# A graph kernel's closing part written out operation by operation, with two additions moved to VectorE

## The chip, the cores and the metric

One core of one Trainium2 chip runs the whole kernel in one launch. The metric is the device time of that core in microseconds (us). Three runs of the kernel before gave 239.44, 239.58 and 240.66 us; their median is 239.58 us.

## The reference, cut to what matters

Two layers over a 0/1 adjacency matrix of 4096 x 4096 and features `x` of 4096 x 64. Each ends in a layer normalisation of the residual sum.

```
# layer 0: neighbours weighted by 0.5^(k - pos), pos = running count of neighbours in the row
w   = mask * where(pos > 0, 0.5 ** (k - pos), 0)
x1  = layernorm(x + w @ (x @ W0) + b0)
# layer 1
deg = max(sum(adj, axis=1) + 1, 1)
z   = concat([x1, (adj @ x1 + x1) / deg]) @ W + b
r   = relu(z)
out = layernorm(x1 + r / max(norm(r, axis=1), 1e-12))
```

Layer 1 needs all rows of `x1`, so the last rows of layer 0 and much of layer 1 are left for the end. That end is what is changed here.

## The kernel before

**Tiling.** The 4096 rows are cut into 8 slabs of 512 (index g), each slab's 4096 neighbours into 8 pieces of 512 (index k). A piece of the transposed adjacency is a bf16 tile of 128 x 4 x 512, brought in by a DMA that GpSimd issues. The main loop walks 64 such pieces. For each it counts neighbours, turns counts into weights (ScalarE line 294, VectorE line 295) and sums layer 0 on TensorE (line 305, `gather`). As soon as a slab's `x1` is known, TensorE also takes in layer-1 sums for other slabs (line 314, `second`), which are set aside in `part`.

**The closing part** begins when the loop ends, at about 193 us of the trace. Slab 7's layer 0 is finished first: `first_hT`, `first_pz` (line 414), then on VectorE the sum y, mean and variance (`moments`, lines 387 and 389), the root (`root_a` and `root_b`, lines 358 to 368) and `x1` (line 441), then a high and a low fp16 half of it (lines 446, 450, 453). The low half is needed by every piece with k = 7.

Next TensorE does the pieces of layer 1 that are left. `own(g, k)` adds one piece to slab g's bank: four matmuls of 512 columns. `own_half(h, k)` (line 608) does the same with 256 columns for half h of slab 7. When a slab has its last piece, `last_hT` (line 627, VectorE) or `half_hT` (line 632, ScalarE) empties the bank into `hT`, and `last_pz` (line 659, TensorE, fp32) multiplies `hT` with the weights.

**A unit** is what follows for one slab, two slabs (4 and 5, 0 and 1) or half of slab 7. Its steps, in order:

- `last_z` (line 664, VectorE) adds the own-row term c1 to the product.
- `last_relu` and `last_sq` (668, 673, ScalarE; 675, VectorE for the halves) and `last_ss` (680, 681, VectorE) give the row's sum of squares.
- `last_rn` gives the inverse norm: a power on GpSimd (line 378), for the halves a root on ScalarE and four small VectorE operations.
- `last_y` (698, VectorE), then `last_add` (703), which adds `x1`: on GpSimd for whole slabs, on VectorE for halves.
- `last_mv`: four or eight times `bn_stats` (387) and then as many `bn_aggr` (389).
- `last_r` (376, 378) and `offset` (736, 737) on GpSimd give scale and offset, `last_o` (748, ScalarE) the output block by block, and `store` (757) hands it to the DMA queue of SP.

Slabs 3 and 7 share one last root (`u37`), so that both wait for the last half; their output is split between VectorE (750) and ScalarE (748).

**What sets the order.** The scheduler is told to keep the written order: each engine executes its instructions in the order in which the closing part calls these functions. Only semaphores stand between the engines. Within one function all instructions of it stand together: the eight `bn_stats` of a unit are issued in one row.

**Buffers.** Small results have tiles of their own from a pool with five buffers for each tag. PSUM banks are kept in a list: a bank emptied goes to the end and the next user takes the first. Outputs and intermediate tiles of the units reuse the buffers of adjacency pieces.

Of the kernel before, what the change touches and what calls it, by code (L numbers as in the profile page):

```python
# [23 lines left out]
P = 128  # L24
# [16 lines left out]
def adj_resnorm_kernel(  # L41
# [583 lines left out]
    def last_hT(g):  # L625
        ep["hT", g] = hT_of(g)
        nc.vector.tensor_tensor(ep["hT", g], acc[g], part[g], ALU.add)  # L627
        banks.append(acc[g])
# [7 lines left out]
    def unit(*slabs):  # L636
        name, bs = "_".join(map(str, slabs)), [g * TB + t for g in slabs for t in range(TB)]
        n = len(bs)
        tiles = []
        for i in range(n // TB):  # L640
            tiles.append(a16p.tile([P, 4 * TB // n, n, D], F32, tag="a16", name=f"u_{name}_{i}"))
        four = [t[:, i] for t in tiles for i in range(4 * TB // n)]
        return name, bs, four

    def half_unit(h):
        _, bs, four = u7
        ts_ = slice(2 * h, 2 * h + 2)
        return f"{L}{'ab'[h]}", bs[ts_], [f[:, ts_] for f in four]

    def rows(bs):  # L650
        return slice(bs[0], bs[-1] + 1)

    def last_pz(u):

        name, bs, _ = u
        pz = ep["pz1", name] = psum(len(bs), D, f"pz1_{name}")
        for t, b in enumerate(bs):
            h = ep["hT", b // TB]
            nc.tensor.matmul(pz[:, t, :], lhsT=h[:, ts(b % TB, P)], rhs=wn_sb, start=True, stop=True)  # L659

    def last_z(u):

        name, bs, (z, _, _, _) = u
        nc.vector.tensor_tensor(z, ep["pz1", name], c1[:, rows(bs), :], ALU.add)  # L664
        free(f"pz1_{name}")

    def last_relu(u):
        nc.scalar.activation(u[2][1], u[2][0], AF.Relu)  # L668

    def last_sq(u):  # L670
        name, bs, (z, sq, _, _) = u
        if len(bs) >= TB:
            nc.scalar.activation(sq, sq, AF.Square)
        else:
            nc.vector.scalar_tensor_tensor(sq, z, 0.0, z, ALU.max, ALU.mult)

    def last_ss(u):
        name, bs, (_, sq, _, _) = u
        ss = ep["ss", name] = small.tile([P, len(bs)], F32, tag="ss", name=f"ss_{name}")
        nc.vector.tensor_reduce(ss, sq, AX.X, ALU.add)  # L680
        nc.vector.tensor_tensor(ss, ss, least[:, rows(bs)], ALU.max)  # L681

    def last_sn(u):
        name = u[0]
        ep["sn", name] = root_a(ep["ss", name], zero, f"n_{name}")

    def last_rn(u):
        name = u[0]
        ss = ep["ss", name]
        if ("sn", name) in ep:  # L690
            ep["rn", name] = root_b(ep["sn", name], ss, zero, f"n_{name}")
        else:
            ep["rn", name] = root_p(ss, None, name, "rn")

    def last_y(u):
        name, bs, (z, _, y, _) = u
        rn = ep["rn", name].unsqueeze(2).to_broadcast([P, len(bs), D])
        nc.vector.scalar_tensor_tensor(y, z, 0.0, rn, ALU.max, ALU.mult)

    def last_add(u):  # L700
        name, bs, (_, _, y, _) = u
        engine = nc.gpsimd if len(bs) >= TB else nc.vector
        engine.tensor_tensor(y, y, x1[:, rows(bs), :], ALU.add)

    mv_37 = small.tile([P, 2 * TB, 2], F32, tag="mv_37", name="mv_37")
    slot_of = {3: 0, L: TB}

    def last_mv(u):
        name, bs, (_, _, y, _) = u
        if bs[0] // TB in slot_of:  # L710
            ep["mv1", "37"] = mv_37
            t = slot_of[bs[0] // TB] + bs[0] % TB
            moments(y, f"l1_{name}", mv_37[:, t : t + len(bs), :])
        else:
            ep["mv1", name] = moments(y, f"l1_{name}")

    def last_s(u):
        name = u[0]
        ep["s1", name] = root_a(ep["mv1", name][:, :, 1], eps_ln, f"l1_{name}")

    def last_r(u):
        name = u[0]
        v = ep["mv1", name][:, :, 1]
        if ("s1", name) in ep:
            ep["r1", name] = root_b(ep["s1", name], v, eps_ln, f"l1_{name}")
        else:
            ep["r1", name] = root_p(v, LN_EPS, name, "r1")

    def offset(u):
        name, bs, _ = u  # L730
        mv, r = ep["mv1", name], ep["r1", name]
        off = ep["off", name] = small.tile([P, len(bs)], F32, tag="off", name=f"off_{name}")
        if ("s1", name) in ep:
            nc.vector.scalar_tensor_tensor(off, mv[:, :, 0], -1.0, r, ALU.mult, ALU.mult)
        else:
            nc.gpsimd.tensor_tensor(off, mv[:, :, 0], r, ALU.mult)
            nc.gpsimd.tensor_scalar(off, off, -1.0, None, ALU.mult)

    def last_o(u, t0, t1, engine=nc.scalar):
        name, bs, (_, _, y, o) = u  # L740
        if bs[0] // TB in slot_of:
            n0 = slot_of[bs[0] // TB]
            mv, r, off = [ep[what, "37"][:, n0 : n0 + TB] for what in ("mv1", "r1", "off")]
        else:
            mv, r, off = ep["mv1", name], ep["r1", name], ep["off", name]
        for t in range(t0, t1):
            if engine is nc.scalar:
                engine.activation(o[:, t, :], y[:, t, :], AF.Identity, bias=off[:, t : t + 1], scale=r[:, t : t + 1])
            else:
                engine.tensor_scalar(  # L750
                    o[:, t, :], y[:, t, :], mv[:, t, 0:1], r[:, t : t + 1], ALU.subtract, ALU.mult
                )

    def store(u):
        name, bs, (_, _, _, o) = u
        for i, b in enumerate(range(0, len(bs), TB)):
            nc.sync.dma_start(out=out[bs[b] // TB], in_=o[:, b : b + TB, :])

    run(NS, DVE)
    gather(*held)  # L760
    own(5, 5)
    first_hT(L)
    banks.append(ps_a.tile([P, R], F32, tag="acc0", name="va0"))
    first_pz(L)
    own(5, 6)
    first_y(L)
    first_mv(L)
    own(4, 6)
    free(f"pz0_{L}")
    first_s(L)  # L770
    own(0, 6)
    first_least(L)
    first_r(L)
    own(1, 6)
    first_x1(L)
    own(2, 5)
    first_hi(L)
    own_half(1, 0)
    first_xl(L)
    own(6, 6)  # L780
    first_lo(L)
    own(6, 7)
    own(4, 7)
    last_hT(6)
    u6 = unit(6)
    last_pz(u6)
    last_hT(4)
    own(5, 7)
    last_z(u6)
    last_relu(u6)  # L790
    own(1, 7)
    last_hT(5)
    last_sq(u6)
    last_ss(u6)
    own(0, 7)
    last_hT(1)
    last_rn(u6)
    u45 = unit(4, 5)
    last_pz(u45)
    last_hT(0)  # L800
    last_y(u6)
    last_add(u6)
    u01 = unit(0, 1)
    last_pz(u01)
    last_z(u45)
    last_mv(u6)
    last_relu(u45)
    last_sq(u45)
    last_r(u6)
    own(2, 7)  # L810
    last_z(u01)
    last_ss(u45)
    own(2, 6)
    last_relu(u01)
    offset(u6)
    last_sq(u01)
    first_px(L)
    last_rn(u45)
    own(3, 7)
    last_hT(2)  # L820
    first_x1T(L)
    free(f"px_{L}")
    last_ss(u01)
    u2 = unit(2)
    last_pz(u2)
    last_o(u6, 2, 4)
    last_o(u6, 0, 2)
    last_y(u45)
    last_rn(u01)
    first_pu(L)  # L830
    last_z(u2)
    store(u6)
    own(3, 6)
    last_relu(u2)
    first_c1(L)
    free(f"pu_{L}")
    last_sq(u2)
    last_add(u45)
    own_half(1, 6)
    last_y(u01)  # L840
    own_half(1, 7)
    last_ss(u2)
    own(3, 5)
    last_add(u01)
    last_mv(u45)
    own_half(1, 1)
    own_half(1, 4)
    last_rn(u2)
    own_half(1, 3)
    own_half(1, 2)  # L850
    last_hT(3)
    own_half(1, 5)
    last_r(u45)
    last_y(u2)
    u3 = unit(3)
    last_pz(u3)
    last_mv(u01)
    half_hT(1)
    u7 = unit(L)
    u7b = half_unit(1)  # L860
    last_pz(u7b)
    own_half(0, 1)
    last_add(u2)
    last_z(u3)
    own_half(0, 7)
    last_z(u7b)
    last_relu(u3)
    own_half(0, 6)
    last_sq(u7b)
    offset(u45)  # L870
    last_ss(u7b)
    own_half(0, 2)
    last_sq(u3)
    last_r(u01)
    own_half(0, 0)
    last_o(u45, 4, 6)
    last_ss(u3)
    own_half(0, 3)
    last_mv(u2)
    last_sn(u7b)  # L880
    own_half(0, 5)
    last_o(u45, 6, 8)
    own_half(0, 4)
    last_rn(u7b)
    last_o(u45, 2, 4)
    last_rn(u3)
    last_y(u7b)
    half_hT(0)
    last_add(u7b)
    last_o(u45, 0, 2)  # L890
    u7a = half_unit(0)
    last_pz(u7a)
    last_y(u3)
    offset(u01)
    last_z(u7a)
    last_add(u3)
# [69 lines left out]
```

## Time and profile before

| | value |
|---|---|
| median of 3 runs | 239.58 us |
| the profiled execution's own time | 239.75 us |
| its span in the trace | 238.0 us |
| outside the span | 1.75 us |
| closing part: last `gather` matmul ends, to the end of the span | 193.13 to 238.0 us |
| busy time in the span: PE, DVE, ACT, POOL | 211.8, 180.1, 136.2, 83.3 us |
| from 193.13 to 227.92 us (34.79 us): PE busy | 32.27 us |
| mean granted TensorE clock over the span | 0.971 |

PE is TensorE, PEld its weight loads, DVE is VectorE, ACT is ScalarE, POOL is GpSimd, SP is the engine that issues the stores. A timeline row gives start, length, engine, line, operation, output and inputs, shapes and the count of instructions in it; in brackets stands the idle time in front of it and who ended it. A row with x4 covers four instructions that follow each other, so that its length divided by four is their spacing and not the duration of one. In the chain of waits, a row gives the part of that work that the end of the span hung on. The granted clock is a share of full speed.

### The profile page before, as it was taken

Reading aid. Unit: us, or ns where it says so; the run is one execution under the profiler, and the core shown is the slowest. Engines: PE = TensorE matmul, PEld = TensorE weight load, DVE = VectorE, ACT = ScalarE, POOL = GpSimd, SP = SyncE. Lnnn points to the kernel's source line nnn. Section 1 sums busy time; section 2 is a strip of 40 time slices with the busy share of each in tenths; the row PEclk is TensorE's granted clock in tenths of the full one; section 3 lists DMA queues with packets and bytes.
Section 4 is the critical chain, followed back from the end, with each engine's and each line's share of the span. In section 5 each row is a group of like instructions: output and inputs, shape, how many; then the busy total and the mean of one; then the engine's idle time right before and its main releaser. Section 6 shows DMA issues by size and latency. Waiting matters only on the chain.

```text
span 238.0 us, 7425 instructions
## 1 busy us (share of the span) xinstructions
PE 211.8 (89%) x3128; PEld 98.4 (41%) x3171; DVE 180.1 (76%) x457; ACT 136.2 (57%) x205; POOL 83.3 (35%) x160
## 2 busy tenths in 40 slices
PE   8689979889997999999999999999999999996920
PEld 2223324234433533443345344434453354765810
DVE  5459788987896699778847975686768765789973
ACT  6058876788676756653655456555645521171582
POOL 8344573432432311213221152214610000277940
PEclk9799999999999999999999999999999999999795
DMA  6999999999999999999999999999930000000021
GB/s 200 209 216 220 212 213 212 222 215 213 220 213 215 214 222 213 212 213 218 218 208 186 193 206 185 187 178 183 196 77 3 3 0 0 3 1 23 3 88 66
DMA packets 11985, 37.34 MB, mean 157 GB/s; under 512 B 1328, under 2 KB 3504, under 8 KB 11952
## 3 DMA queue, kind: packets, MB, share of 16 engines
q0 software_dynamic: 9216, 33.56, 72.4%
q1 hardware_dynamic: 2736, 3.31, 4.5%
q8 instruction: 25, 0.41, 0.6%
q14 instruction: 8, 0.07, 0.1%
HBM read 69.37 MB, written 1.05 MB: 296 GB/s over the span
## 4 chain that ended last, share of the span: by engine, by line
PE 47%; DMA 34%; issue 7%; DVE 7%; POOL 2%; ACT 2%; ACTq 0%; POOLq 0%
DMA a<-in_adjT_dram 34%; PE acc L305 11%; PE acc_part L314 10%; PE v L278 5%; PE cnt L248 4%; PE v L287 3%; PE va L659 2%; PE va L314 2%; PE vb L608 2%; PE pi L528 2%; PE rep L266 1%; PE vb L314 1%; PE ma L314 1%; PE pz L414 1%; ACT w L294 1%
## 5 line engine op out<-in xcount | busy, mean ns | idle before, releaser
L294 ACT ACTIVATE w<-v,less 128x1024 int16<-128x1024 f32 x64 | 71.3, 1113 | 50.4 <-PE v L287 38.0
L295 DVE TENSOR_SCALAR w<-v 128x1024 int16<-128x1024 f32 x64 | 78.2, 1222 | 19.1 <-PE v L287 17.7
L105 POOL DMA_DIRECT2D a<-in_adjT_dram x64 | 35.8, 560 | 97.0 <-PE rep L266 34.4
L305 PE MATMUL acc<-w,xhl 128*128 128x512 bf16 x240 | 66.1, 379 | 2.1 <-issue 1.1
L314 PE MATMUL acc_part<-a,x1hl 128*128 128x512 bf16 x132 | 37.3, 381 | 2.1 <-issue 1.4
L305 PEld LDWEIGHTS <-xhl 128*128 128x128 f16 x256 | 23.1, 98 | 32.7 <-issue 9.1
L268 ACT ACTIVATE near<-rep,most 128x512 bf16<-128x512 f32 x39 | 26.6, 682 | 8.2 <-PE rep L266 8.1
L314 PEld LDWEIGHTS <-x1hl 128*128 128x128 f16 x224 | 18.6, 98 | 30.4 <-issue 14.4
L278 PE MATMUL v<-a,tri 32*32 32x512 bf16 x1024 | 28.7, 385 | 0.5 <-ACT w L294 0.5
L287 PE MATMUL v<-near,mine 32*32 32x512 bf16 x1024 | 27.7, 376 | 0.0
L248 PE MATMUL cnt<-a,pick 128*32 128x512 bf16 x256 | 21.2, 386 | 6.5 <-DMA a<-in_adjT_dram 4.9
L258 DVE TENSOR_TENSOR cs<-cnt,cs 128x512 bf16<-128x512 f32 x31 | 21.2, 685 | 6.4 <-PE cnt L248 6.3
L278 PEld LDWEIGHTS <-tri 32*32 32x32 bf16 x1024 | 9.7, 88 | 19.7 <-issue 19.3
L378 POOL TENSOR_TENSOR rn<-ss,power 128x4 f32<-128x4 f32 (+1 forms) x5 | 6.3, 1276 | 29.0 <-DVE ss L681 28.9
L266 PE MATMUL rep<-cs,further 128*128 128x512 bf16 x39 | 15.0, 385 | 1.0 <-DVE cs L258 1.0
L248 PEld LDWEIGHTS <-pick 128*32 128x32 bf16 x256 | 6.0, 94 | 21.5 <-issue 12.6
L233 POOL TENSOR_TENSOR a<-a,ident_b 128x128 bf16<-128x128 bf16 x32 | 12.7, 429 | 0.1
L287 PEld LDWEIGHTS <-mine 32*32 32x32 bf16 x1024 | 10.3, 87 | 2.5 <-issue 2.4
L659 PE MATMUL va<-wts,hT 128*128 128x64 f32 x64 | 8.8, 292 | 2.4 <-DVE hT L627 1.9
L260 DVE CAST cs<-cnt 128x512 bf16<-128x512 f32 x8 | 5.5, 691 | 6.7 <-PE cnt L248 6.7
L659 PEld LDWEIGHTS va<-wts,hT 128*128 128x128 f32 x64 | 8.4, 206 | 3.7 <-DVE hT L627 2.8
L668 ACT ACTIVATE u<-u 128x256 f32<-128x256 f32 (+1 forms) x5 | 2.5, 502 | 12.4 <-DVE u L664 12.4
(136 smaller groups left out, 241.5 us busy)
## 6 DMA issues: line engine op xcount, KB each, us to landing
a<-in_adjT_dram POOLq DMA_DIRECT2D x64, 512.0 KB, 16.5
c<-in_x_quads_dram SPq DMA_DIRECT2D x2, 512.0 KB, 4.5
x<-in_x_dram SPq DMA_DIRECT2D x8, 128.0 KB, 7.3
out_dram<-u SPq DMA_DIRECT2D x8, 128.0 KB, 1.7
wts<-in_weights_dram SPq DMA_DIRECT2D x1, 160.0 KB, 7.2
```

The source lines that it names most:

```text
L105: nc.gpsimd.dma_start(out=a, in_=adjT[g, k])
L248: nc.tensor.matmul(cnt[g][quarters[q], :], lhsT=pick[:, PW - 4 * k : PW - 4 * k + Q], rhs=A[g][k][:, q, :], start=first, stop=last,)
L258: nc.vector.tensor_tensor(new, cnt[g], cs[g], ALU.add)
L266: nc.tensor.matmul(pr, lhsT=further, rhs=cs[g], start=True, stop=True)
L268: nc.scalar.activation(near[g], pr, AF.Relu, bias=most, scale=-1.0)
L278: nc.tensor.matmul(v[e // 2][quarters[q], e % 2, :], lhsT=tri[quarters[e], :], rhs=A[g][k][quarters[e], q, :], start=True, stop=False,)
L287: nc.tensor.matmul(v[e // 2][quarters[q], e % 2, :], lhsT=mine[quarters[e], 4 * k + q, :], rhs=nr[quarters[e], :], start=False, stop=True,)
L294: nc.scalar.activation(w[:, 0:2, :], v[0], AF.Relu, bias=less)
L295: nc.vector.tensor_scalar(w[:, 2:4, :], v[1], -STEP * MAX_NEIGH, 0.0, ALU.add, ALU.max)
L305: nc.tensor.matmul(acc0[g], lhsT=xhl[:, b, :], rhs=w[:, q, :].bitcast(BF16), start=(k, q) == (NK - 1, 0), stop=(k, q) == (0, KB - 1),)
L314: nc.tensor.matmul(acc, lhsT=x1hl[:, b, :], rhs=A[g][b // KB][:, b % KB, :], start=first, stop=last)
L659: nc.tensor.matmul(pz[:, t, :], lhsT=h[:, ts(b % TB, P)], rhs=wn_sb, start=True, stop=True)
```

## The change

The calls of the closing part are replaced by a table `work` of named single operations and a written `order` of names; each name is issued once, in that order. So the instructions of one unit no longer stand together: `bn_stats` and `bn_aggr` of several units are mixed with each other and with additions, and the pieces of TensorE come in another sequence. The arithmetic is the same with three differences: the sum `y + x1` of slabs 2 and 3 goes from GpSimd to VectorE (`DVE_ADDS`); GpSimd takes the sign of the mean as a first step and multiplies by the scale afterwards (before: product, then sign); of slab 7's last four blocks VectorE does three and ScalarE one (before two and two). All small results lie in one tile `scratch`, in columns of their own. The store of slab 3 is issued in front of slab 7's (before: behind it). The main loop is not touched.

```diff
-    def last_add(u):
-        name, bs, (_, _, y, _) = u
-        engine = nc.gpsimd if len(bs) >= TB else nc.vector
-        engine.tensor_tensor(y, y, x1[:, rows(bs), :], ALU.add)
...
-            nc.gpsimd.tensor_tensor(off, mv[:, :, 0], r, ALU.mult)
-            nc.gpsimd.tensor_scalar(off, off, -1.0, None, ALU.mult)
...
+    scratch = a16p.tile([P, KB * R // 2], F32, tag="a16", name="scratch")
+    taken = [0]
+    def little(n, m=None):
+        v = scratch[:, taken[0] : taken[0] + n * (m or 1)]
+        taken[0] += n * (m or 1)
+        return v if m is None else v.rearrange("p (n m) -> p n m", m=m)
...
+    def statistics(name, y, mv):
+        st = little(mv.shape[1], 6)
+        for t in range(mv.shape[1]):
+            work[f"bn_{name}_{t}"] = lambda t=t: nc.vector.bn_stats(st[:, t, :], y[:, t, :])
+            work[f"ag_{name}_{t}"] = lambda t=t: nc.vector.bn_aggr(mv[:, t, :], st[:, t, :])
...
+    UNITS = ['6', '45', '01', '2', '3', '7b', '7a']
+    COPIED = ()
+    DVE_ADDS = ('2', '3', '7b', '7a')
+    SHARED = ('3', '7b', '7a')
...
+        adder = nc.vector if u in DVE_ADDS else nc.gpsimd
+        work["add" + u] = lambda: adder.tensor_tensor(y, y, x1[:, rows, :], ALU.add)
+        statistics(u, y, mv)
...
+                by_dve = tt >= (1 if u in halves else 2)
...
+        work["eps" + u] = lambda: nc.gpsimd.tensor_scalar(r1, mv[:, :, 1], LN_EPS, None, ALU.add)
+        work["pow" + u] = lambda: nc.gpsimd.tensor_tensor(r1, r1, power[:, 0:n], ALU.pow)
+        work["neg" + u] = lambda: nc.gpsimd.tensor_scalar(off, mv[:, :, 0], -1.0, None, ALU.mult)
+        work["of" + u] = lambda: nc.gpsimd.tensor_tensor(off, off, r1, ALU.mult)
...
+    order = """
+        gather own5_6 fhT fpz own0_6 y0 bn_L0_3 bn_L0_0 own1_6 bn_L0_1 bn_L0_2 ag_L0_0 ag_L0_2 ag_L0_3 ag_L0_1
+        deg s0 own2_6 qa_r0 qb_r0 qc_r0 least qd_r0 own5_5 x1_1 x1_2 x1_3 x1_0 own6_6 least2 hi xl own4_6 lo
+        own6_7 own4_7 hT6 own5_7 hT4 pz6 hT5 pz45 z6 relu6 sq6 ss6 own0_7 ssm6 z45 rn6 own1_7 relu45 hT0 y6 sq45
+        px ownha_6 hT1 add6 x1T ownha_0 ss45 pz01 ssm45 bn_6_1 rn45 ag_6_1 bn_6_0 ag_6_0 bn_6_2 ag_6_2 bn_6_3 pu
+        ag_6_3 z01 own2_5 eps6 y45 relu01 pow6 own2_7 t1 sq01 c1 own3_6 add45 ss01 own3_5 hT2 ssm01 bn_45_5 rn01
+        bn_45_6 pz2 bn_45_3 bn_45_4 ag_45_3 bn_45_2 bn_45_1 bn_45_0 own3_7 ag_45_0 ag_45_6 ag_45_4 ag_45_1 z2
+        y01 neg6 ownha_2 relu2 of6 ownhb_5 o6_1 ag_45_5 ag_45_2 add01 bn_45_7 sq2 ownha_4 ag_45_7 hT3 o6_2
+        ownhb_1 o6_0 ss2 pz3 o6_3 eps45 ssm2 bn_01_6 bn_01_0 st6_0 rn2 bn_01_5 bn_01_7 ownha_7 bn_01_2 ag_01_7
+        bn_01_1 ownha_5 ag_01_6 z3 neg45 ownha_1 y2 relu3 pow45 bn_01_4 ownhb_0 bn_01_3 sq3 add2 ownha_3 bn_2_0
+        bn_2_2 ownhb_4 ag_2_0 bn_2_1 hT7a ss3 pz7a of45 ssm3 bn_2_3 o45_1 ag_01_5 rn3 ownhb_3 ag_01_1 ag_01_2
+        ag_01_3 ag_01_0 o45_0 ag_01_4 ag_2_3 ownhb_6 ag_2_1 z7a o45_5 ownhb_7 sq7a o45_2 eps01 y3 ownhb_2 o45_3
+        neg01 ss7a pow01 o45_7 st45_0 ssm7a ag_2_2 add3 hT7b sn7a bn_3_0 pz7b o45_6 bn_3_2 bn_3_1 bn_3_3 o45_4
+        qa_n7a z7b qb_n7a st45_4 of01 sq7b qc_n7a o01_3 neg2 ss7b eps2 ag_3_1 o01_0 ag_3_0 ssm7b ag_3_3 pow2
+        qd_n7a sn7b y7a o01_5 qa_n7b add7a o01_4 qb_n7b bn_7a_0 o01_7 qc_n7b of2 ag_7a_0 bn_7a_1 qd_n7b o2_3 y7b
+        o2_0 ag_7a_1 ag_3_2 add7b o2_2 bn_7b_1 bn_7b_0 o01_6 ag_7b_1 ag_7b_0 sS st01_4 o01_2 qa_S qb_S o2_1 qc_S
+        o01_1 qd_S st2_0 offS o7_3 o3_1 st01_0 o3_3 o3_2 o3_0 o7_1 o7_0 st3 o7_2 st7
+    """
     run(NS, DVE)
...
+    for name in order.split():
+        work.pop(name)()
```

The names: `ownG_K` a piece of slab G, `ownha_K` and `ownhb_K` of slab 7's first and second half, `hTU` the emptying of a bank, `pzU` the fp32 product, then `zU`, `reluU`, `sqU`, `ssU` and `ssmU` (sum of squares and its floor), `rnU` (inverse norm by GpSimd's power) or `snU` and `qa_` to `qd_` (by a root), `yU`, `addU`, `bn_` and `ag_` (statistics), `epsU`, `powU`, `negU`, `ofU` (scale and offset), `oU_T` one output block, `stU` a store. `sS`, `qa_S` to `qd_S` and `offS` are the root and offset shared by slabs 3 and 7.

## The prediction

> **What bounds the kernel now.** I read the share of slices first: the only slices in which TensorE is neither busy nor at full clock lie at the end, so the closing part from 193.13 us was read row by row. TensorE's timeline there has one long hole:
>
> ```profile
> 215.81 2.35 PE L608 MATMUL mb<-a,x1hl 128*128 128x256 bf16 x20
> 220.09 2.32 PE L659 MATMUL va<-wts,hT 128*128 128x64 f32 x12 [1.94 <-DVE hT L627]
> 222.21 4.58 PE L608 MATMUL vb<-a,x1hl 128*128 128x256 bf16 x32
> 227.25 0.66 PE L659 MATMUL va<-wts,hT 128*128 128x64 f32 x4 [0.46 <-ACT hT L632]
> ```
>
> TensorE stood 1.94 us for the emptying of slab 3's bank. Its work behind the hole was also slow: 32 matmuls of 256 columns took 4.38 us in the chain, where the 20 in front took 2.35 us with the pipeline's end (109 ns apart). The windows (PE's busy time, then the granted clock) say why:
>
> ```profile
> 218.50:219.50 1.00, 0.00 (x0) 1.00 0.00 0
> 220.50:221.50 1.00, 1.00 (x8) 0.58 0.00 0
> 221.50:222.50 1.00, 1.00 (x7) 0.50 0.00 0
> 222.50:223.50 1.00, 1.00 (x7) 0.50 0.00 0
> 223.50:224.50 1.00, 1.00 (x8) 0.71 0.00 0
> 224.50:225.50 1.00, 1.00 (x11) 1.00 0.06 16
> ```
>
> Why was the bank emptied late? The chain that ended last runs through VectorE in front of it:
>
> ```profile
> 214.71 1.76 DVE u L698
> 216.47 0.34 DVE ss L680
> 216.81 0.02 issue
> 216.84 1.07 DVE ss L681
> 217.90 1.02 DVE st_l L387 x8
> 218.92 0.54 DVE mv_l L389 x8
> 219.47 0.58 DVE hT L627
> ```
>
> Two rows are too long: line 698 on 128x512 takes 0.69 us elsewhere, line 681 takes 0.16. And 16 statistics stand in front of line 627, though TensorE needs that one. GpSimd's timeline shows what ran beside the two long rows:
>
> ```profile
> 214.51 1.41 POOL L703 TENSOR_TENSOR u<-u,x 128x512 f32<-128x512 f32 x1
> 216.62 1.27 POOL L703 TENSOR_TENSOR u<-u,x 128x512 f32<-128x512 f32 x1 [0.69 <-DVE u L698]
> ```
>
> Line 681 ends with the second addition, line 698 about half a microsecond after the first.
>
> **What the Trainium skill says.** SBUF — State Buffer, section Who interferes with whom: a VectorE instruction with two SBUF inputs and a GpSimd instruction that reads SBUF exclude each other, and the later one waits for all of the earlier; one with a single SBUF input, and a reduction, do not. The two rows above agree, and so does line 627 (one input in PSUM), which took its usual 0.69 us during GpSimd work. GpSimd's powers do not show it: line 681 took 0.17 us at 212.57 inside a power of 1.64 us. TensorE: Matmul & The Clock Gate, section What's actually happening: an idle window of about 3.4 us halves the clock. Here 1.94 us were enough; the low clock lasted about 3.4 us. The same page, Architectural detail, has VectorE and ScalarE as strict queues, which the trace bears out: nothing overtakes. VectorE: DVE Perf Modes, The DRAIN you can't avoid, holds that a wait between two VectorE operations costs nothing extra. This trace differs: independent `bn_stats` follow each other every 128 ns though one lasts 208, while each step of a root starts only 20 to 30 ns after its predecessor's end. So mixing steps of different units saves some 0.1 us a step.
>
> **The change, part by part.** I wrote down the new order for each engine and walked it with the rows of before: an instruction starts when its engine is free and its inputs are there, plus the 0.03 to 0.08 us that the trace shows between engines. Spacings: piece 0.862, half piece 0.436, fp32 product of a slab 0.88 (two blocks alone 0.66), output block on ScalarE 0.345, `bn_aggr` 0.067.
>
> *TensorE, same instructions in another sequence.* The end of the gather stays at 193.13. The first trap is own6_7, which needs the low half of x1: its VectorE and ScalarE steps are unchanged (ready at 200.06), and one piece, the product of 0.99 and six pieces bring TensorE to 200.17, so nothing is lost, with 0.1 us to spare (before: 0.5). Then three pieces and 12 blocks of product (205.5), two pieces, transpose 0.22 and two halves (208.3), product of slabs 0 and 1 (210.1), pu 0.23, four pieces, product of slab 2 (214.65), own3_7 (215.5) and four halves: TensorE comes to pz3 at 217.3. It needs hT3. On VectorE z2 runs 214.9 to 215.3, y01 waits for rn01 (GpSimd, ready 215.36) and ends at 216.1, three small statistics follow, hT3 runs 216.4 to 217.1. So the hole of 1.94 us closes, with 0.15 us to spare, because statistics of units 0 and 1 now stand behind hT3. With the hole goes the low clock: 3.4 us at half clock is 1.7 us of work. Six halves, pz7a (its wait for hT7a hides behind the sixth, ownhb_4) and four halves end at 223.2; hT7b (0.37 on ScalarE, whose six output blocks in front of it are through at 223.2) and 0.66 us of product end at 224.3, before 227.92. Gain up to here: 1.94 + 1.7 = 3.64 us, and the wait of about 0.46 us for the last hT stays.
>
> *The additions.* Adding x1 to slabs 2 and 3 costs VectorE 2 x 0.42 us (the row of c1, same shape and inputs) and frees GpSimd of 2 x 0.73. The two left on GpSimd lie, in the walk, at 212.2 to 213.5 and 216.15 to 217.4. Beside them VectorE has reductions, statistics and bank emptyings; only ssm01 and ssm2 have two SBUF inputs and come right at their end. So about 2.0 us of blocking (1.76 - 0.69 and 1.07 - 0.16) become at most 0.2. That feeds the closing of the hole and is not counted again.
>
> *GpSimd.* Its list of powers and offsets, 19.57 us busy from 205.58 before, loses 1.46 and keeps 18.1; with 0.07 us between instructions and 1 to 1.5 us of waits it ends at 226.6 instead of 229.5. The sign in front of the power costs nothing and gains nothing by itself, since GpSimd does its four steps in a row either way: it moves 0.25 us from behind the power to in front of it. Where the mean waits for nothing, that is a gain of 0.25 us for the first output block; where GpSimd is the late engine, zero. I take zero.
>
> *The tail.* From z7b (224.34): square, sum, floor 225.4; root on ScalarE 225.8; four small operations 226.56; y, add, two `bn_stats`, two `bn_aggr` 227.75. The shared root sS is ready to start at 227.8, but on ScalarE it stands behind seven output blocks (225.75 + 7 x 0.345 = 228.2). Root 0.3, four small operations, offset: 229.6. Then three blocks on ScalarE: 230.75. Before, the same point was 235.05 and the span ended 2.95 us later (store issue 0.33, landing 1.7, end). The other stores are issued earlier than before, and slab 3's just ahead of slab 7's, which finds SP's queue free again 0.33 us later, about when its last block is done. So the span would end at 233.7. Against the 3.64 us above this is 0.66 us more: one ScalarE block fewer at the end (0.34), and slab 3's statistics no longer between floor and root (about 0.4), less the wait of sS.
>
> *Sum.* 238.0 - 3.64 - 0.66 = 233.7. The walk has almost no slack on three engines at once, and none of its small hand-offs was allowed to be late. I add 0.4 us for that: a choice, about a dozen hand-offs at 0.03. Span 234.1, plus 1.75 outside gives 235.85 for an execution like the profiled one, which lay 0.17 above the median: **235.7**.
>
> **The rivals.** *(B) GpSimd becomes the bound.* Offset of slab 2 is ready at 226.6 and ScalarE wants it at 226.8; sS queues behind it. If GpSimd runs 1 to 2 us later than walked, sS and the end move by nearly as much: 236.7 to 238.3, say 237.2. For it: 18 of 20.8 us busy. Against: before, it had 4.4 us of idle in its list, so its rows are true durations. *(C) The hole comes back smaller,* at pz3 or at pz01, where the product needs hT1: an idle time of 1.5 to 2 us with the low clock again leaves only the tail's 0.7 and some of the addition's: 238.4 to 240. *(D) Slower.* hT3 stands behind y01, and y01 behind GpSimd's pow6, add45 and rn01. If these run 2.5 us later than walked, TensorE waits 2.4 us at 217.3, and its remaining 7 us begin with 3.4 us at half clock (1.7); with about 1 us that the late engines add to the tail this comes to 5.1: 240.8. A delay below some 2.4 us doesn't make it slower than before. Against it: GpSimd's two powers in front are 1.05 and 1.64 in five and four rows, with little spread. *(E) One shared tile makes engines wait for each other.* If dependencies were kept for the tile and not for columns, VectorE's statistics would wait for GpSimd's powers. In the built order they wait only for VectorE and for the addition; I leave it within D.
>
> **Chances.** Walk as described 0.68 (own range 234.6 to 236.6), B 0.19, C 0.07, D with E 0.06. The range 234.6 to 237.8 leaves out C, D, the end of B and a little below. Half a per cent, about what a measurement of this kernel can tell, is 1.2 us: faster means under 238.4. Faster 0.87, same 0.07, slower 0.06.
>
> **What would show it.** Right: no idle time of over 0.7 us on PE from 193 to 224 and clock 1.00 there; PE's last product at about 224.3; GpSimd's last row at 226 to 227; sS on ScalarE near 228.2; no VectorE row on line 777 over 0.8 us or on 776 over 0.3. Wrong: a hole in front of a line 757 product with a clock near 0.5 after it, or VectorE idle for GpSimd in front of y.

## The result

The kernel after takes 237.04 us, the median of seven runs (236.68 to 238.51); seven runs of the kernel before on the same chip gave 239.58 (238.34 to 240.66). The ratio is 0.9919, with a 95% interval of 0.9892 to 0.9946: faster, by 2.5 us between the medians or about one per cent. Ratios, intervals and spans here and below are taken from the fast runs of each kernel, so that a ratio is not the quotient of the two medians beside it. In a later series it was 236.93 us against 239.82, a ratio of 0.9869 (0.9834 to 0.9905). The forecast was 235.7, a gain of 3.9 us in a range of 234.6 to 237.8.

The profiled execution took 238.51 us with a span of 235.0; the spans of the others are 234.7 to 235.8, so its closing part is a typical one, and only the time outside the span is long in it. In the kernel after, line 757 is the fp32 product, 710 and 715 empty the banks, 777 is y, 775 and 776 the sum of squares and its floor, 774 the inverse norm's power, 781 the addition, 804 to 807 the steps `eps`, `pow`, `neg` and `of` of GpSimd, 788 the output, 768 a half's root, 827 the shared root, and 649 and 650 `bn_stats` and `bn_aggr`.

The granted clock in the page of the kernel after, in 40 slices:

```profile
PEclk9999999999999999999999999999999999999995
```

TensorE's timeline of the kernel after (start, length, engine, line, operation, tiles and shapes, count; idle time in front):

```profile
217.73 1.10 PE L757 MATMUL vb<-wts,hT 128*128 128x64 f32 x8 [0.24 <-DVE hT L710]
...
221.97 1.91 PE L608 MATMUL vb<-a,x1hl 128*128 128x256 bf16 x16
224.48 0.66 PE L757 MATMUL va<-wts,hT 128*128 128x64 f32 x4 [0.60 <-ACT hT L715]
```

The hole of 1.94 us is 0.24 us, and the 16 matmuls of 256 columns behind it run 109 ns apart, as they do in front of it. The windows of the kernel after (length, busy time of PE, PEld, DVE, ACT and POOL, granted clock, DMA share, GB/s) show no slow clock behind it:

```profile
217.00:221.00 4.00, 3.76 (x35) 3.23 (x33) 3.80 (x21) 2.57 (x7) 3.83 (x5) 1.00 0.09 33
221.00:224.00 3.00, 2.86 (x25) 2.12 (x22) 2.75 (x20) 2.30 (x7) 2.76 (x6) 1.00 0.00 0
```

TensorE's last product ends at 225.14, 2.8 us earlier than before and 0.8 later than I had walked. VectorE is hardly held by GpSimd's additions any more. Its timeline in the kernel after:

```profile
211.00 0.68 DVE L777 SCALAR_TENSOR_TENSOR u<-u,scratch 128x512 f32<-128x512 f32 x1
...
213.63 0.53 DVE L776 TENSOR_TENSOR scratch<-scratch,least 128x8 f32<-128x8 f32 x1
...
215.92 0.69 DVE L777 SCALAR_TENSOR_TENSOR u<-u,scratch 128x512 f32<-128x512 f32 x1
...
217.01 0.66 DVE L710 TENSOR_TENSOR hT<-va,part 128x512 f32<-128x512 f32 x1
```

The two y over 512 columns take 0.68 and 0.69 us (one took 1.76 before). Of the two floors, the one of units 0 and 1 takes 0.53 us, because it stands for GpSimd's addition that ends at 214.14; in the kernel before it was slab 2's floor that stood, for 1.07 us, and that one takes 0.16 now. Now read GpSimd's timeline of the kernel after against the starts of those rows:

```profile
210.99 0.79 POOL L804 TENSOR_SCALAR scratch<-scratch 128x4 f32<-128x4 f32 x1
...
215.97 0.74 POOL L806 TENSOR_SCALAR scratch<-scratch 128x4 f32<-128x4 f32 x1
...
219.64 0.48 POOL L806 TENSOR_SCALAR scratch<-scratch 128x8 f32<-128x8 f32 x1
...
223.09 0.48 POOL L804 TENSOR_SCALAR scratch<-scratch 128x8 f32<-128x8 f32 x1
223.65 0.24 POOL L806 TENSOR_SCALAR scratch<-scratch 128x8 f32<-128x8 f32 x1
223.86 1.92 POOL L805 TENSOR_TENSOR scratch<-scratch,power 128x8 f32<-128x8 f32 x1
...
227.75 0.20 POOL L807 TENSOR_TENSOR scratch<-scratch 128x4 f32<-128x4 f32 x1
```

These small operations take 0.23 to 0.25 us where no y of VectorE runs beside them (223.65). Beside a y they take 0.79, 0.74, 0.48 and 0.48, and all four end 0.10 us after that y ends (210.99 + 0.79 = 211.78, y 211.68). The power at 223.86 lasts 1.92 us instead of 1.66; beside its start VectorE's addition ran (223.87, 0.39 us). So GpSimd now stands for VectorE, where VectorE stood for GpSimd before. Its list ends at 227.95, 1.35 us later than I had walked. The chain that ended last in the kernel after runs through it:

```profile
214.24 1.65 POOL scratch L774
215.89 0.08 issue
215.97 0.74 POOL scratch L806
...
223.89 1.90 POOL scratch L805
...
226.09 0.77 ACT u L788 x2
226.86 0.19 ACT scratch L768
227.05 2.37 ACT u L788 x7
229.42 0.28 ACT scratch L827
```

GpSimd's offset of units 0 and 1 (226.06) releases two output blocks on ScalarE; behind them stand the root of the last half, seven further blocks and, at 229.4, the shared root on which slabs 3 and 7 wait. Before, TensorE's late bank stood in that chain.

### The profile page after: what moved, and what is told of

Same layout as the page of the kernel before. It is cut to its first block, busy times and chain, and to the rows that moved or that the text cites. A ratio compares the mean times of both kernels' runs of the same rounds, so it can differ in the third digit from the quotient of the medians.

```text
span 235.0 us, 7423 instructions
## 1 busy us (share of the span) xinstructions
PE 209.6 (89%) x3128; PEld 96.9 (41%) x3171; DVE 179.8 (77%) x460; ACT 135.9 (58%) x204; POOL 82.6 (35%) x158
## 4 chain that ended last, share of the span: by engine, by line
DMA 38%; PE 37%; issue 7%; DVE 7%; POOL 6%; ACT 4%; ACTq 0%; POOLq 0%
DMA a<-in_adjT_dram 38%; PE acc L305 9%; PE acc_part L314 9%; PE v L278 4%; PE cnt L248 3%; PE v L287 2%; ACT u L788 2%; DVE w L295 2%; POOL scratch L774 2%; PE vb L314 2%; POOL scratch L805 2%; POOL a L105 1%; ACT w L294 1%; PE va L757 1%; DVE x L441 1%
## 5 line engine op out<-in xcount | busy, mean ns | idle before, releaser
L774 POOL TENSOR_TENSOR scratch<-scratch,power 128x4 f32<-128x4 f32 (+1 forms) x5 | 6.4, 1277 | 29.1 <-DVE scratch L776 29.0
L788 ACT ACTIVATE u<-u,scratch 128x64 f32<-128x64 f32 x27 | 9.8, 428 | 2.2 <-POOL scratch L807 2.1
L446 ACT CAST x1hl<-x 128x256 f16<-128x256 f32 x8 | 3.2, 404 | 10.9 <-DVE x L441 8.9
```

The costliest lines, as they stand in the source:

```text
L788: nc.scalar.activation(o[:, t, :], y[:, t, :], AF.Identity, bias=off[:, t : t + 1], scale=r[:, t : t + 1])
```

## The experiments

The theory after the result: the gain is the closed hole, its clock and a re-ordered end, and GpSimd's standing took back about 1.2 us of the forecast. Its rivals: a single move of the old order would have brought most of it; or the additions did. Each kernel below was timed against the kernel before on the same chip, in three series on three chips: the first four rows; then the kernel after repeated, additions on GpSimd, z kept in PSUM and offset on VectorE; then the other four. Kernels of different series are compared by their ratios.

| kernel | median us | ratio to before | 95% interval |
|---|---|---|---|
| before, hT3 early | 239.23 | 0.9988 | 0.9967 to 1.0009 |
| before, hole filled | 238.82 | 0.9965 | 0.9947 to 0.9983 |
| before, additions on VectorE | 239.78 | 0.9995 | 0.9967 to 1.0023 |
| before, hT3 early and additions | 239.01 | 0.9982 | 0.9962 to 1.0002 |
| before, three moves | 239.39 | 1.0010 | 0.9995 to 1.0026 |
| after, repeated | 236.93 | 0.9869 | 0.9834 to 0.9905 |
| after, additions on GpSimd | 239.99 | 1.0012 | 0.9984 to 1.0040 |
| after, hT3 late | 240.95 | 1.0025 | 0.9992 to 1.0059 |
| after, z kept in PSUM | 236.95 | 0.9875 | 0.9836 to 0.9914 |
| after, z kept, bank chosen | 237.14 | 0.9912 | 0.9884 to 0.9940 |
| after, offset on VectorE | 236.69 | 0.9851 | 0.9819 to 0.9883 |
| after, both of these | 237.08 | 0.9898 | 0.9860 to 0.9936 |

### Is it the hole? hT3 moved forward in the old order

```diff
     own(3, 5)
+    last_hT(3)
...
-    last_hT(3)
     u3 = unit(3)
     last_pz(u3)
```

> The kernel before with one instruction moved: slab 3's bank is emptied ahead of the 16 statistics of slabs 4 and 5, nothing else. Theory (the hole in TensorE with its low clock is what the change removed, and GpSimd's list takes over as the bound at the end): hole at the product of slab 3 under 0.6 us instead of 1.94, clock 1.00 behind it, TensorE's last product ends near 224.8 instead of 227.9; but GpSimd's list still ends at 229.5 or a little later, ScalarE's outputs of slab 2 and the shared root behind them come at about 230.9 instead of 232.2, so only 1.3 us of 3.1 reach the end: about 238.2. Rival (the gain comes from mixing the small steps of all units, not from this hole): unchanged at 239.5 to 239.7.

Measured: 239.23 us. The hole went, the gain did not come. TensorE's timeline of this kernel:

```profile
218.16 1.55 PE L659 MATMUL va<-wts,hT 128*128 128x64 f32 x12 [0.39 <-DVE hT L627]
219.55 3.66 PE L608 MATMUL vb<-a,x1hl 128*128 128x256 bf16 x32
225.70 0.66 PE L659 MATMUL va<-wts,hT 128*128 128x64 f32 x4 [2.50 <-ACT hT L632]
```

The 32 matmuls take 3.66 us instead of 4.58, but in front of the last product stands a new wait of 2.50 us: the wait moved from VectorE to ScalarE. ScalarE's timeline shows what the copy stood behind:

```profile
223.12 0.77 ACT L748 ACTIVATE u<-u,off,r 128x64 f32<-128x64 f32 x2 [0.37 <-POOL off L737]
...
223.98 1.42 ACT L748 ACTIVATE u<-u,off,r 128x64 f32<-128x64 f32 x4
225.30 0.35 ACT L632 COPY hT<-vb 128x256 f32<-128x256 f32 x1
```

Output blocks of slabs 4 and 5, which wait for GpSimd's offset, are written ahead of the copy, and so TensorE waits for them, and for GpSimd through ScalarE's queue. My expectation of 238.2 missed that.

### Is it the clock? The hole filled with work

Eight matmuls of 512 columns, whose result nothing uses, stand in front of slab 3's product; nothing else moves.

```diff
     u3 = unit(3)
+    for i in range(8):
+        nc.tensor.matmul(banks[0], lhsT=x1hl[:, i, :], rhs=A[L][7][:, 3, :], start=True, stop=True)
     last_pz(u3)
```

> The kernel before with eight extra matmuls of 512 columns (some 1.7 us of work whose result is not used) on TensorE in front of the product of slab 3, where the hole was. Theory (the low clock comes from the idle time in front of it): clock 1.00 from 218 to 227, the hole itself stays as lost time, TensorE's last product ends near 226.2, 1.7 us earlier; at the end 1.0 to 1.5 us of it arrive: about 238.3. Rival (the low clock has another cause than idle time): clock still near 0.5 for some 3.4 us, time 239.6 or more.

TensorE's timeline of this kernel:

```profile
217.93 1.89 PE L857 MATMUL va<-a,x1hl 128*128 128x512 bf16 x8
220.02 1.55 PE L659 MATMUL va<-wts,hT 128*128 128x64 f32 x12 [0.20 <-DVE hT L627]
221.41 3.66 PE L608 MATMUL vb<-a,x1hl 128*128 128x256 bf16 x32
225.55 0.66 PE L659 MATMUL va<-wts,hT 128*128 128x64 f32 x4 [0.49 <-ACT hT L632]
```

The product starts no earlier than before (220.02, before 220.09), yet the 32 matmuls take 3.66 us, and the last product ends at 226.21 instead of 227.92. So it is TensorE's idleness that lowers the clock. The time is 238.82, 0.9 us better. In these two executions that is half of the 1.7 us on TensorE; a middle execution has less than 1.7 to win (estimated at 1.2 us below).

### Is it the additions? In the old order, with and without hT3

```diff
-        engine = nc.gpsimd if len(bs) >= TB else nc.vector
+        engine = nc.gpsimd if len(bs) >= TB and bs[0] // TB not in (2, 3) else nc.vector
```

> The kernel before with the additions of x1 for slabs 2 and 3 on VectorE, in the old order. Theory (GpSimd is not the bound as long as the hole is there): the hole and the low clock stay, GpSimd's list ends 1.3 to 1.5 us earlier (about 228.1), the end hardly moves: 239.2 to 239.8. Rival (the additions are what the change gained by): 237 to 238.3.

> The kernel before with both edits: slab 3's bank emptied ahead of the 16 statistics, and the additions of slabs 2 and 3 on VectorE. Theory: TensorE's last product near 224.8 and GpSimd's list near 228.2, the shared root on ScalarE at 229.5 to 230: about 237.2, so as good as the whole change. Rival (the mixing of small steps is worth something of its own): 1 us or more behind the changed kernel, 238 to 239.

Alone: 239.78, nothing gained. TensorE's timeline of that kernel has the hole and the slow clock:

```profile
220.42 1.55 PE L659 MATMUL va<-wts,hT 128*128 128x64 f32 x12 [1.93 <-DVE hT L627]
221.81 5.32 PE L608 MATMUL vb<-a,x1hl 128*128 128x256 bf16 x32
```

Together with the early hT3: 239.01, where my theory wanted 237.2. TensorE's last product in that kernel waits as it did in the first experiment:

```profile
226.06 0.66 PE L659 MATMUL va<-wts,hT 128*128 128x64 f32 x4 [2.35 <-ACT hT L632]
```

The rival, that the rest of the order is worth a microsecond or more, holds. Of the additions only this is shown: moved alone they are free, and bring nothing.

### Three moves on two engines of the old order

hT3 early as above; the copies of slab 7's first half ahead of the outputs of slabs 4 and 5; the shared root ahead of slab 2's outputs.

```diff
     own(3, 5)
+    last_hT(3)
...
-    last_o(u45, 4, 6)
-    last_o(u45, 6, 8)
-    last_o(u45, 2, 4)
...
     half_hT(0)
+    last_o(u45, 4, 6)
+    last_o(u45, 6, 8)
+    last_o(u45, 2, 4)
...
     last_s(u37)
+    last_o(u2, 0, 2)
+    last_o(u2, 2, 4)
```

> The kernel before with three moves and no arithmetic changed: slab 3's bank emptied ahead of the 16 statistics; on ScalarE the emptying of slab 7's first half ahead of the outputs of slabs 4 and 5; the last shared root ahead of slab 2's four outputs. Theory (what moving the first hole alone did not bring is lost in ScalarE's queue, where the emptying stood 2.5 us behind outputs): TensorE's last product near 223.9 to 224.5, no wait over 0.6 us in front of it, the shared root at 229.6 to 230.3, end 1.3 us or so better than the one move: 237.4 to 238.2. Rival (only the mixing of small steps brings the rest): 239.0 to 239.3.

Measured: 239.39, a clear miss. TensorE did all that was asked of it:

```profile
218.65 1.55 PE L659 MATMUL va<-wts,hT 128*128 128x64 f32 x12 [0.40 <-DVE hT L627]
...
224.33 0.66 PE L659 MATMUL va<-wts,hT 128*128 128x64 f32 x4 [0.64 <-ACT hT L632]
```

It is done at 224.99, 2.9 us earlier than before and even earlier than in the kernel after. The timelines of GpSimd, VectorE and ScalarE, put together by time, show where this went:

```profile
225.62 1.01 POOL L378 TENSOR_TENSOR rn<-ss,power 128x4 f32<-128x4 f32 x1
226.66 0.43 DVE L698 SCALAR_TENSOR_TENSOR u<-u,rn 128x256 f32<-128x256 f32 x1 [0.30 <-POOL rn L378]
227.01 0.28 DVE L664 TENSOR_TENSOR u<-va,c 128x128 f32<-128x128 f32 x1
227.33 0.78 DVE L675 SCALAR_TENSOR_TENSOR u<-u 128x128 f32<-128x128 f32 x1
...
228.66 0.30 ACT L358 ACTIVATE s_n_7a<-ss_7a,zero 128x2 f32<-128x2 f32 x1
...
231.73 0.30 ACT L358 ACTIVATE s_l<-mv,eps_ln 128x8 f32<-128x8 f32 x1 [1.45 <-DVE mv L389]
```

The product that TensorE has ready at 224.99 is taken up by VectorE (line 664) at 227.01 only. In VectorE's queue slab 3's y (line 698) stands in front of it, and that waits for slab 3's power on GpSimd (225.62), which has slab 2's addition ahead of it in GpSimd's queue. Then the half's square (line 675) takes 0.78 us instead of the 0.29 of the kernel before, beside GpSimd's addition of slab 3 (227.24, 0.72 us). So the half's root starts at 228.66, VectorE's last statistics come late, and the shared root starts at 231.73 (before 232.19). In the old order, then, TensorE's 3 us are worth next to nothing by themselves: the wait moved to VectorE's queue, and GpSimd's behind it.

### One part undone: additions back on GpSimd, hT3 late again

```diff
-    DVE_ADDS = ('2', '3', '7b', '7a')
+    DVE_ADDS = ('7b', '7a')
```

> The changed kernel, with the additions of x1 to slabs 2 and 3 back on GpSimd, at the same places of the order. Theory (GpSimd is the bound of the end): its list grows by 2 x 0.73 us and ends near 229.2, the shared root starts 1.0 to 1.4 us later: about 238.2. Rival (the additions don't matter, as in the old order): 237.0 to 237.3.

Measured: 239.99. All 3 us are gone, more than I expected. VectorE's timeline of this kernel:

```profile
222.19 0.35 DVE L649 BATCH_NORM_STATS2 scratch<-u 128x6 f32<-128x64 f32 x2 [2.20 <-POOL u L781]
...
227.60 0.60 DVE L649 BATCH_NORM_STATS2 scratch<-u 128x6 f32<-128x64 f32 x4 [2.30 <-POOL u L781]
```

and GpSimd's:

```profile
219.81 1.66 POOL L805 TENSOR_TENSOR scratch<-scratch,power 128x8 f32<-128x8 f32 x1
221.43 0.73 POOL L781 TENSOR_TENSOR u<-u,x 128x256 f32<-128x256 f32 x1
...
226.85 0.72 POOL L781 TENSOR_TENSOR u<-u,x 128x256 f32<-128x256 f32 x1
```

Each addition stands behind a power of 1.66 us in GpSimd's queue, and VectorE, whose statistics of that slab come next in its written order, stands still for 2.20 and 2.30 us. The same choice that brought nothing in the old order is worth the whole gain in the new one: here the statistics of slabs 2 and 3 are written soon after the addition, and all that VectorE still has to do stands behind them. This shows what the new order needs, not that additions on GpSimd are slow in every order.

In the other kernel, hT3 and slab 3's product go behind ten further statistics (the expectation below says nine) and slab 2's sum and floor, much as in the old order:

```diff
-        y01 neg6 ownha_2 relu2 of6 ownhb_5 o6_1 ag_45_5 ag_45_2 add01 bn_45_7 sq2 ownha_4 ag_45_7 hT3 o6_2
-        ownhb_1 o6_0 ss2 pz3 o6_3 eps45 ssm2 bn_01_6 bn_01_0 st6_0 rn2 bn_01_5 bn_01_7 ownha_7 bn_01_2 ag_01_7
-        bn_01_1 ownha_5 ag_01_6 z3 neg45 ownha_1 y2 relu3 pow45 bn_01_4 ownhb_0 bn_01_3 sq3 add2 ownha_3 bn_2_0
+        y01 neg6 ownha_2 relu2 of6 ownhb_5 o6_1 ag_45_5 ag_45_2 add01 bn_45_7 sq2 ownha_4 ag_45_7 o6_2
+        ownhb_1 o6_0 ss2 o6_3 eps45 ssm2 bn_01_6 bn_01_0 st6_0 rn2 bn_01_5 bn_01_7 bn_01_2 ag_01_7
+        bn_01_1 ag_01_6 bn_01_4 bn_01_3 hT3 pz3 ownha_7 ownha_5 z3 neg45 ownha_1 y2 relu3 pow45 ownhb_0 sq3 add2 ownha_3 bn_2_0
```

> The changed kernel with the emptying of slab 3's bank put behind nine further statistics on VectorE, nothing else. Theory (this instruction's place is worth the hole and the clock behind it): TensorE idle 2 to 2.6 us at the product of slab 3, clock near 0.5 for some 3.4 us behind it, the last product 3.5 to 4 us later (near 228.8), end 2.5 to 3.5 us later: about 240. Rival (the other queues have slack that takes it in): 237 to 238.

Measured: 240.95. TensorE's timeline has a hole larger than that of before:

```profile
219.96 1.10 PE L757 MATMUL vb<-wts,hT 128*128 128x64 f32 x8 [2.74 <-DVE hT L710]
```

The gain is gone here too (ratio 1.0025, 0.9992 to 1.0059), so the hole's closing was necessary as well. But in this execution, the fastest one of this kernel (238.66), a window behind the hole shows a full clock (columns as above):

```profile
222.00:224.00 2.00, 1.98 (x19) 1.56 (x16) 1.93 (x16) 1.13 (x4) 0.49 (x1) 1.00 0.00 0
```

Whether the clock falls behind such a hole varies from execution to execution. The span and mean granted clock of each timed execution bear it out:

| kernel | executions | standard deviation of the span, us | correlation of span and clock |
|---|---|---|---|
| before (three series) | 115 | 0.83 | -0.73 |
| before, additions on VectorE (hole) | 13 | 0.78 | -0.59 |
| after, hT3 late (hole) | 12 | 0.99 | -0.70 |
| before, hole filled | 22 | 0.46 | 0.05 |
| before, hT3 early | 14 | 0.43 | -0.02 |
| before, three moves | 22 | 0.31 | 0.16 |

With the hole, the executions with a low clock are the long ones; without it the scatter halves and the clock says nothing. Two kernels with other waits on TensorE lie in between: additions on GpSimd (14 executions, 0.55 us, -0.37) and z kept in PSUM (6 executions, 0.56 us, -0.73). A tenth of the executions of before have a span of up to 236.7 us, the middle one has 237.9; I take the difference, 1.2 us, as an estimate of what the clock costs a middle execution. It is too high as far as the scatter has other causes; filling the hole brought 0.9.

### What did GpSimd's standing cost?

In four units z is written over its product in PSUM (`zz()` is that bank for the units in `KEPT`), and y and the relu step read it there, so that y has only one SBUF input; the bank is given back after y.

```diff
-            nc.vector.tensor_tensor(z, ep["pz1", u], c1[:, rows, :], ALU.add)
-            free(f"pz1_{u}")
+            nc.vector.tensor_tensor(zz(), ep["pz1", u], c1[:, rows, :], ALU.add)
+            if u not in KEPT:
+                free(f"pz1_{u}")
...
+    KEPT = ('45', '01', '2', '3')
```

> The changed kernel itself again, as the yardstick for the three beside it: 236.7 to 237.4.

> The changed kernel, with z of all whole slabs left in its PSUM bank until y has been formed, so that y has one SBUF input instead of two. Theory (the long small rows of GpSimd, 0.79, 0.74, 0.48 and 0.48 us where 0.25 is usual, are GpSimd standing for y, which reads two SBUF inputs): these four rows fall to about 0.25, GpSimd's list ends near 226.5 instead of 227.95, the shared root on ScalarE starts about 1 us earlier, end 0.7 to 1.2 us earlier: about 236.0. Rival (GpSimd's small rows are long for a reason of its own): rows and time unchanged.

GpSimd's timeline of this kernel, the four rows that took 0.79, 0.74, 0.48 and 0.48 us:

```profile
211.00 0.25 POOL L814 TENSOR_SCALAR scratch<-scratch 128x4 f32<-128x4 f32 x1
...
216.57 0.26 POOL L816 TENSOR_SCALAR scratch<-scratch 128x4 f32<-128x4 f32 x1
...
220.04 0.27 POOL L816 TENSOR_SCALAR scratch<-scratch 128x8 f32<-128x8 f32 x1
...
223.28 0.25 POOL L814 TENSOR_SCALAR scratch<-scratch 128x8 f32<-128x8 f32 x1
```

The y beside them start within 0.05 us of them, as in the kernel after, but now have one SBUF input. So the cause of the rows' length is shown. The time is 236.95 against 236.93: in this kernel slabs 2 and 3 share a PSUM tile, which opened a wait of 0.79 us on TensorE at slab 2's product, and GpSimd's list again ended at 227.75. With slab 3's bank taken from another place in the list:

```diff
-            acc[g] = banks.pop(0)
+            acc[g] = banks.pop(3 if g == 3 else 0)
```

> As a_zpsum (z of whole slabs stays in PSUM until y), with the bank of slab 3 chosen so that slabs 2 and 3 do not sum in the two halves of one PSUM tile, as they came to do in a_zpsum. Theory (y's two SBUF inputs delay GpSimd, and GpSimd's lateness sets the end): the small GpSimd rows stay at 0.25, no wait of VectorE for TensorE of 0.87 us in front of slab 2's emptying, GpSimd's list ends 1.0 to 1.5 us earlier than in the changed kernel, end 0.6 to 1.1 us earlier: about 236.1. Rival (the end hangs on VectorE's chain of slab 7 or ScalarE's outputs as much as on GpSimd): GpSimd earlier, end within 0.3 us of 236.93.

GpSimd's list ended at 226.46, 1.2 us earlier than in the repeated kernel after (227.69), and the hole at slab 3's product was gone. The time: 237.14, with a ratio of 0.9912 no better than the kernel after. TensorE's timeline shows a wait for the bank of a kept z:

```profile
223.36 0.60 PE L608 MATMUL vb<-a,x1hl 128*128 128x256 bf16 x4 [0.58 <-DVE u L764]
```

The third way takes offset's two steps from GpSimd and makes them one VectorE instruction; the last kernel joins it with the kept z.

```diff
-        work["neg" + u] = lambda: nc.gpsimd.tensor_scalar(off, mv[:, :, 0], -1.0, None, ALU.mult)
-        work["of" + u] = lambda: nc.gpsimd.tensor_tensor(off, off, r1, ALU.mult)
+        work["of" + u] = lambda: nc.vector.scalar_tensor_tensor(off, mv[:, :, 0], -1.0, r1, ALU.mult, ALU.mult)
```

> The changed kernel, with the offset of slabs 6, 4 and 5, 0 and 1, and 2 formed in one VectorE instruction each instead of two on GpSimd. Theory (GpSimd's list is the bound of the end): GpSimd ends 2 to 2.5 us earlier, ScalarE's outputs come earlier, the shared root is then held by VectorE's last statistics or by ScalarE's own queue: end 0.6 to 1.0 us earlier, about 236.2. Rival (ScalarE's queue of outputs or VectorE is the bound, GpSimd only looks it): within 0.3 us of the changed kernel.

> Both relief measures for GpSimd together: z in PSUM until y, and the offsets by one VectorE instruction each. Theory: GpSimd ends near 224.5, nothing waits for it any more; what is left is TensorE's last product, the chain of slab 7's second half and ScalarE's outputs: 235.6 to 236.2. Rival: no better than the offsets alone (236.69).

Measured: 236.69, with GpSimd done at 226.19 and the shared root at 229.21 (repeated kernel after 229.14); and 237.08, with GpSimd done at 225.8 and the shared root at 229.57. GpSimd relieved by up to 2 us gives at most 0.24 us, which the intervals do not separate. So GpSimd alone is not the bound of the kernel after: TensorE's last product and VectorE's steps for slab 7's last half, which follow it, end almost as late.

## Why the prediction was right, and where its size failed

**The hole and the clock: right.** TensorE waits 0.24 us at slab 3's product (forecast: none over 0.7), the clock is 1.00, and the experiment with dummy matmuls shows the link between the two. But the term "3.4 us at half clock is 1.7 us" was read from one execution: the estimate above is 1.2 us for the middle one.

**The additions: right in what they no longer hold, wrong in which way the exclusion works.** My step ran: beside GpSimd's additions VectorE has nothing with two SBUF inputs except the two floors, so "about 2.0 us of blocking become at most 0.2". For VectorE that nearly came out: y at 0.68 and 0.69, but one floor 0.36 us too long (0.53). The Trainium skill, SBUF — State Buffer, section Who interferes with whom, makes the shared ports an exclusive lock and lets the order of issue decide which of the two engines is blocked. I had priced only VectorE as the blocked one. GpSimd's small reads are blocked as well, and not by chance: each of these y is released by a power's end, and GpSimd starts its next operation 0.08 us after it (215.89 and 215.97), 0.05 behind y. This case's numbers agree: 0.74 us, and 0.26 with one input in PSUM.

**GpSimd's list: the term that was mis-sized.** "It ends at 226.6" was 227.95. Four small operations and a power took about 1.7 us more than their rows of before (0.53 + 0.49 + 0.23 + 0.23 + 0.26). In "against B" I wrote that its rows are true durations; they were true for the old neighbours only. The timelines of before even had one row of the new kind, which I passed over (GpSimd, then VectorE):

```profile
226.16 0.53 POOL L737 TENSOR_SCALAR off<-off 128x8 f32<-128x8 f32 x1
...
226.17 0.42 DVE L698 SCALAR_TENSOR_TENSOR u<-u,rn 128x256 f32<-128x256 f32 x1
```

Line 737 takes 0.24 to 0.26 us elsewhere, and here too GpSimd ends 0.10 us after the y. The extra 0.53 at 211 went on to the addition behind it (212.87), to the floor of 0.53, to the power at 214.24, to y at 215.92 and to hT3 at 217.01: that is the 0.24 us hole.

**The tail: 1.2 us late, in two queues.** The shared root was walked to 228.2 and started at 229.40; from there to the end of the span it is 5.6 us (walked 5.5). One side is ScalarE: the offset of units 0 and 1 came at 226.06, and nine output blocks and a root had to follow. The other side is VectorE, whose statistics were ready at 229.36 (walked 227.75): TensorE's last product ended 0.84 late (0.43 at slab 3's product, of which 0.13 came from the main loop, 0.25 over the spacings behind it, the rest on ScalarE's copy), the half's root stood 0.45 us behind output blocks, and VectorE's chain from there took 2.31 us instead of 1.95. The two sides met within 0.1 us. They are not independent, for the blocks in front of the half's root waited for GpSimd's offset.

**The sum.** Span 235.2 in the median run against 234.1 forecast (the 0.4 us for hand-offs was too little by 1.1), and 1.84 us outside it against 1.6: 237.04 against 235.7. So the walk's own range (234.6 to 236.6) missed, and the whole range held because rival B was in it: GpSimd 1 to 2 us late with 236.7 to 238.3 us, to which I gave 0.19, is nearest to what happened. That much of being right is luck. Of the signs, the hole, the clock and line 777 came out; TensorE's last product, GpSimd's last row, the shared root and line 776 (0.53 against at most 0.3) did not. As the only bound B is refuted by the last experiment. C, D and E are not seen. A small misreading: a root's steps start 30 to 40 ns after their predecessor's end (229.95 + 0.22, then 230.21), not 20 to 30.

**Where the gain lies.** I booked it as 3.64 us on TensorE and 0.66 in the tail. The profiled executions, one for each kernel, can be cut at two points, the end of TensorE's last product and the start of the shared root (all in us; the execution of before has the low clock, that of hT3 late has not):

| kernel | gather's end to last product's end | from there to the shared root | from there to the end |
|---|---|---|---|
| before | 34.77 | 4.28 | 5.81 |
| before, hT3 early | 33.61 | 4.87 | 5.77 |
| before, three moves | 31.77 | 6.74 | 5.87 |
| after | 31.88 | 4.26 | 5.60 |
| after, additions on GpSimd | 32.44 | 6.64 | 5.64 |
| after, hT3 late | 34.26 | 3.92 | 5.64 |
| after, z kept, bank chosen | 32.11 | 3.92 | 5.60 |
| after, offset on VectorE | 31.81 | 4.00 | 5.59 |

The gain is on TensorE: 2.89 us against the 3.64 booked, and 0.23 behind it. But the three moves win 3.00 us there as well and lose 2.46 in the second stretch, and additions on GpSimd lose 2.38 there: in both kernels VectorE stands behind something of GpSimd's. What the change gains is thus TensorE's time together with an order that lets it through VectorE's and ScalarE's queues, and each of the two parts that were undone lost the whole gain. The table also says why relief of GpSimd gave so little. No kernel has a second stretch below 3.92 us, so that the kernel after has about 0.34 us to win there (an estimate from these rows), and the kept z lost 0.23 of it on TensorE. Against the walk (31.17, 3.9 and 5.5) the kernel after is late by 0.71, 0.36 and 0.10 us.

The clock alone is not the gain either. Even the fastest of 115 executions of before (span 236.4), with a mean clock of 0.986, is 1.7 us behind the fastest of after (234.7); that part is the hole and the order of the other engines.

**Open.** What GpSimd's standing costs in all, since each kernel that removed it opened another wait; what the other block split, the sign taken first and the order of the stores are worth, which no run undoes (in the table the last stretch is 0.21 us shorter with them); and whether a few more moves of the old order would have reached the new one. Three moves joined with the additions were not tried, though both of GpSimd's additions stand in the way of slab 7's last half in the three moves' timelines.

## What to carry to other kernels

When a move closes a hole on the busiest engine, follow what stands in each in-order queue between that engine and the last store, and ask for each late result which queue holds it: here single repairs brought 0 to 0.9 us and the whole order 2.5 to 2.9. A duration from a trace holds for its neighbours, and an exclusion between two engines has to be priced in both directions, above all where the one's end releases the other. Where two queues end within 0.1 us of each other, as here, relief of one gave nothing that could be measured.

## What was not expected of the hardware

- The clock fell behind an idle time of 1.94 us in the profiled execution of before, and behind 2.74 us it stayed at 1.00 in the profiled execution of the kernel with hT3 late. The Trainium skill, TensorE: Matmul & The Clock Gate, section What's actually happening, has a free-running window of activity of about 3.4 us. The variation between executions fits a window that runs free, though no run here shows the window itself; that less than a window of idle time is enough does not fit its wording, and the measurement decides.
- Filling a hole with useless matmuls made the kernel before 0.9 us faster (ratio 0.9965, 0.9947 to 0.9983).
- GpSimd's powers show little of the exclusion. The power of units 4 and 5 (220.09, 1.66 us) had a VectorE addition of two SBUF inputs inside it (220.19, 0.41 us), and both took their usual time; the power at 223.86 took 1.92 us, and there the addition began with it (223.87). It looks as if a power were held for its reading at the start only; no run was made for that.
